# Activations and attention transposed in 32x32 blocks on VectorE and placed by DMA, in place of transposes on TensorE

## The chip, the core and the metric

The kernel runs on one core of one Trainium2 chip. The metric is device time in microseconds (us), median of several executions. Every execution told of here is marked fast in the record, and the results were correct. In both kernels TensorE (PE) multiplies into PSUM; VectorE (DVE) and ScalarE (ACT) evict PSUM and do elementwise work; GpSimd (POOL) does elementwise work in SBUF; all DMAs are issued, in order, from the queue of SyncE (SPq). Issue is the time that a DMA holds that queue; it has landed when its data may be read. A run of bytes is a contiguous piece that a DMA moves.

## The reference, cut to what matters

```python
h = relu(layernorm(x))                       # x: 128 batches x 64 tokens x 768, f32
for l in range(2):
    m_left, m_right = h @ W_left[l].T, h @ W_right[l].T
    u = (upper triangle of h @ m_left.T, lower triangle of h @ m_right.T) / sqrt(768)
    e = exp(u) * adj
    attention = e / (e.sum(2) + 1e-10)       # 64 x 64 per batch
    ctx = attention @ (h @ W_lin[l].T + b_lin[l])
    h = relu(layernorm_std(ctx) * ln_a[l] + ln_b[l])
return x + h
```

## The kernel before

Sixteen blocks of 512 tokens (8 batches) go through two passes per layer. Pass one needs `h` transposed (hidden index on partitions): it projects left and right in groups of seven products (Strassen-like sums of tokens and weights, PSUM banks X, Y, Z, V), and forms the scores and the attention. Pass two does the linear layer, the context and the layer norm.

The order of emission matters, since each engine runs its instructions in order (in block 0 VectorE stood 3.72 us for x, and TensorE 1.82 us for an eviction behind that). Side work is put in a queue of small closures, one of which is emitted after every product (`pump(1)`; an empty closure in the queue, an empty turn, a spacer, only delays what follows it):

```python
def project(u, k, g, between=None):
    for i, (at, a, t) in enumerate(ORDER):    # X Y Z V X Z V
        ...                                   # 3 matmuls into bank `at`
        if i == 0:   nc.scalar.copy(s1, p)
        elif i == 1: nc.vector.tensor_add(u2, p, s1)
        elif i == 2: nc.vector.tensor_add(u4, p, u2)      # bank Z is read here ...
        elif i == 4: nc.scalar.copy(to, pb)
        else:        nc.vector.tensor_add(to, pb, ...)    # ... and i == 5 adds into bank Z
        if i == 1 and between: between()      # scores(u - 1), queues its chain
        pump(1)

# per block, in pass one:
for g in range(CH):
    project(u, 0, g, (lambda: scores(u - 1)) if u and g == 0 else None)
    if g == 0:
        load(u + 1)                           # x (layer 0) or h (layer 1), adjacency
        prepare(u + 1)                        # queues the work on the next block
for g in range(CH): project(u, 1, g)

# prepare, layer 0: statistics and normalization on VectorE, then
for c in range(2):
    for q in range(Q):
        nc.tensor.transpose(p[:, c, q*P:(q+1)*P], xr[q][:, (c0+c)*P:(c0+c+1)*P], ident)
nc.scalar.activation(ht[:, c0:c0+2, :], p, AF.Relu)

# last links of the score chain (seven links): normalize, four transposes, one store
nc.tensor.transpose(pt[:, q, :], bd[:, q, :], ident)
nc.scalar.copy(at, pt)
nc.sync.dma_start(ATT[l][u], at)
```

In pass two of layer 0 each half block is transposed on TensorE, scaled and shifted by ScalarE on its way out of PSUM, and stored; pass one of layer 1 loads it as it needs it.

## Time and profile before

| | before |
|---|---|
| median time | 3039.55 us (3038.8 to 3040.02, 3 runs; 3039.78 with a fourth, run beside the changed kernel) |
| TensorE busy | 3001.1 us, 99% of the span |
| VectorE, ScalarE, GpSimd busy | 35%, 18%, 25% |
| mean granted TensorE clock | 0.998 |
| DMA packets | 77,994, 244.66 MB |

In a timeline line the first two numbers are start and duration in us; then engine, source line, operation, output and inputs, the number of instructions merged, and in brackets how long the engine had stood idle and what ended it.

### The profile page before, as it was taken

What the parts mean: (1) busy time and instruction counts of PE and PEld (TensorE: products, weight loads), DVE (VectorE), ACT (ScalarE), POOL (GpSimd) and SP (SyncE); (2) the same over time, 40 slices, a digit from 0 to 9 for tenths busy, and PEclk for the clock granted to TensorE, in tenths of its full rate; (3) what the DMA queues carried; (4) which work ended last, traced back from release to release, by engine and by line L of the source; (5) the groups of instructions that cost most, each with busy time, mean ns of one, the idle gap of its engine ahead of it and who ended that gap; (6) DMA issues with size and microseconds to landing.
All of it is one profiled execution on the core that took longest, in us unless ns stands there. A gap on an engine that the chain in (4) does not pass through costs nothing.

```text
span 3039.2 us, 37771 instructions
## 1 busy us (share of the span) xinstructions
PE 3001.1 (99%) x15744; PEld 2328.2 (77%) x15744; DVE 1061.3 (35%) x2231; ACT 551.6 (18%) x1124; POOL 765.5 (25%) x486
## 2 busy tenths in 40 slices
PE   7999999999999999999999999999999999999998
PEld 6888888888888755555568888888888886555554
DVE  4333333433333222222223222222222224555555
ACT  1112111121111144343431000000000001111111
POOL 3311211111112152322323111111111112555554
PEclk9999999999999999999999999999999999999999
DMA  4211211112111132222221010001000102444444
GB/s 173 80 56 49 90 49 49 56 49 91 49 49 61 53 152 111 98 107 111 90 90 60 29 56 28 28 29 56 28 28 29 56 28 100 152 177 153 177 152 139
DMA packets 77994, 244.66 MB, mean 81 GB/s; under 512 B 8448, under 2 KB 34560, under 8 KB 67584
## 3 DMA queue, kind: packets, MB, share of 16 engines
q1 hardware_dynamic: 77824, 242.25, 21.9%
q8 instruction: 124, 2.03, 0.3%
q14 instruction: 46, 0.38, 0.0%
HBM read 158.34 MB, written 83.89 MB: 80 GB/s over the span
## 4 chain that ended last, share of the span: by engine, by line
PE 97%; DVE 1%; DMA 1%; ACT 0%; issue 0%; POOL 0%; DVEq 0%; POOLq 0%; ACTq 0%; SPq 0%
PE Z L259 16%; PE V L259 16%; PE X L259 16%; PE Y L259 8%; PE Z L497 8%; PE V L497 8%; PE X L497 8%; PE aux L293 6%; PE Y L497 4%; PE aux L417 3%; PE aux L470 1%; PE aux L226 1%; PE aux L323 0%; DMA x<-in_x_dram 0%; DVE bd L317 0%
## 5 line engine op out<-in xcount | busy, mean ns | idle before, releaser
L135 POOL TENSOR_TENSOR ts<-ht 128x768 f32<-128x768 f32 x126 | 238.7, 1894 | 1541.3 <-ACT ht L228 742.7
L259 PE MATMUL X<-ht,w_l_A 128*128 128x256 f32 x1152 | 281.3, 380 | 0.0
L259 PE MATMUL V<-ts,w_l_A 128*128 128x256 f32 x1152 | 280.2, 379 | 0.5 <-DVE n L280 0.5
L259 PE MATMUL X<-ht,w_r_A 128*128 128x256 f32 x1152 | 280.0, 379 | 0.0
L259 PE MATMUL V<-ts,w_r_A 128*128 128x256 f32 x1152 | 280.0, 379 | 0.0
L497 PE MATMUL X<-w_n_A,ht 128*128 128x384 f32 x768 | 269.0, 486 | 0.3 <-DVE s L502 0.3
L497 PE MATMUL V<-w_n_A,ts 128*128 128x384 f32 x768 | 268.7, 486 | 0.0
L280 DVE TENSOR_TENSOR n<-V,u 128x256 f32<-128x256 f32 x384 | 162.3, 423 | 278.2 <-PE V L259 277.0
L259 PEld LDWEIGHTS X<-ht,w_r_A 128*128 128x128 f32 x1152 | 218.9, 190 | 29.8
L259 PEld LDWEIGHTS V<-ts,w_r_A 128*128 128x128 f32 x1152 | 218.9, 190 | 29.8
L135 POOL TENSOR_TENSOR ts<-ht,ts 128x768 f32<-128x768 f32 x126 | 239.3, 1899 | 7.7 <-ACT ht L228 6.4
L259 PEld LDWEIGHTS X<-ht,w_l_A 128*128 128x128 f32 x1152 | 218.4, 191 | 29.1
L259 PEld LDWEIGHTS V<-ts,w_l_A 128*128 128x128 f32 x1152 | 217.5, 190 | 30.0 <-DVE n L280 1.2
L273 DVE TENSOR_TENSOR u<-Y,s 128x256 f32<-128x256 f32 x192 | 81.5, 425 | 408.4 <-PE Y L259 408.4
L497 PEld LDWEIGHTS X<-w_n_A,ht 128*128 128x128 f32 x768 | 143.3, 190 | 94.0 <-DVE s L502 0.9
L497 PEld LDWEIGHTS V<-w_n_A,ts 128*128 128x128 f32 x768 | 143.5, 190 | 93.5
L280 DVE TENSOR_TENSOR n<-Z,u 128x256 f32<-128x256 f32 x192 | 80.8, 421 | 381.7 <-PE Z L259 381.7
L278 ACT COPY n<-X 128x256 f32<-128x256 f32 x192 | 71.5, 373 | 745.3 <-PE X L259 745.3
L435 ACT ACTIVATE z<-aux 128x768 f32<-128x768 f32 x128 | 102.6, 807 | 566.5 <-PE aux L417 566.5
L507 POOL TENSOR_TENSOR u2b<-u,b 128x384 f32<-128x384 f32 x64 | 63.8, 998 | 551.0 <-DVE u L505 551.0
L270 ACT COPY s<-X 128x256 f32<-128x256 f32 x192 | 71.5, 373 | 619.9 <-PE X L259 619.9
L293 PEld LDWEIGHTS aux<-n,ht 128*64 128x64 f32 x3072 | 167.0, 137 | 10.6 <-issue 10.6
(104 smaller groups left out, 4003.4 us busy)
## 6 DMA issues: line engine op xcount, KB each, us to landing
ht<-h SPq DMA_DIRECT2D x48, 1536.0 KB, 6.7
x<-in_x_dram SPq DMA_DIRECT2D x64, 384.0 KB, 7.2
h<-ht SPq DMA_DIRECT2D x16, 1536.0 KB, 6.1
h<-n SPq DMA_DIRECT2D x16, 1536.0 KB, 5.0
xr<-in_x_dram SPq DMA_DIRECT2D x64, 384.0 KB, 4.2
out_dram<-xr SPq DMA_DIRECT2D x64, 384.0 KB, 2.3
att<-at SPq DMA_DIRECT2D x32, 256.0 KB, 2.0
at<-att SPq DMA_DIRECT2D x32, 256.0 KB, 7.0
```

Source lines behind the costliest of these rows:

```text
L135: queue.append(lambda o=o, m=m, n=n: eng.tensor_sub(b[o], b[m], b[n]))
L226: nc.tensor.transpose(p[:, c, q * P:(q + 1) * P], xr[q][:, (c0 + c) * P:(c0 + c + 1) * P], ident)
L259: nc.tensor.matmul(p, w[a][:, c, g * P:(g + 1) * P], b[t][:, c, :], start=(new and c == 0), stop=(c == CH - 1), skip_group_check=True)
L270: nc.scalar.copy(s1, p)
L273: nc.vector.tensor_add(u2, p, s1)
L278: nc.scalar.copy(to, pb)
L280: nc.vector.tensor_add(to, pb, (u4 if i == 3 else u2).rearrange("p (b s) -> p b s", s=S))
L293: nc.tensor.matmul(p[h * S:(h + 1) * S, q, :], ht[:, c, b * S:(b + 1) * S], m[c // CH][:, c % CH, b].rearrange("p k j -> p (k j)"), start= ...
L417: nc.tensor.matmul(cx[k][i, m, :HH], at[j, q, j], hl[j, q, m * HH:(m + 1) * HH], start=True, stop=True)
L435: nc.scalar.activation(zs[k].rearrange(two, n=2), cx[k], AF.Square, accum_out=ss[:, k:k + 1])
L497: nc.tensor.matmul(p, b[t][:, c, r * P:(r + 1) * P], w[a][:, c, :], start=(new and c == 0), stop=(c == CH - 1), skip_group_check=True)
L507: nc.gpsimd.tensor_add(u2b, u2, rows["b2"])
```

## The change

The intent: TensorE is the bound, so take its 872 transposes off it. VectorE transposes 32x32 blocks, and DMAs to DRAM and back put the blocks in place. Only the first block of layer 0 keeps its TensorE transposes. The batches in a block are laid out anew so that the blocks fit.

```diff
+    def transpose_rows(l, u, pool):                  # layer 0 after statistics and relu
+        for q in range(Q):
+            queue.append(lambda q=q: nc.vector.transpose(
+                xb[:, :, q, :], xr[q].rearrange("p (b j) -> p b j", j=32)))
+        queue.append(store)                          # four DMAs, 512 byte runs
+        queue.append(lambda: load_h(1, l, u))        # one DMA back
+        queue.extend([lambda: None] * 4)             # four empty turns
+        affine(1, l, u)                              # layer 1: six ScalarE activations
...
-                    pt = ps_aux.tile(...)            # attention, last links
-                    for q in range(Q):
-                        nc.tensor.transpose(pt[:, q, :], bd[:, q, :], ident)
-                    nc.scalar.copy(at, pt)
-                    nc.sync.dma_start(ATT[l][u], at)
+                    nc.vector.transpose(at..., v...)
+                    for a in range(4):
+                        for g in range(2):
+                            nc.sync.dma_start(to[a // 2, a % 2, g], at[a * 32:(a + 1) * 32, g])
                 it = chain()
-                for _ in range(7):
+                for _ in range(6):
...
-                    nc.sync.dma_start(t, x_t[u][q])  # x: four DMAs of 128 partitions
+                    for a in range(4):               # eight DMAs of 32 partitions
+                        nc.sync.dma_start(t[a * 32:(a + 1) * 32], src.rearrange("(k j) h -> j k h", k=2))
...                                                  # pass two, layer 0
-                queue.append(lambda c0=c0: turn(c0)) # TensorE transposes, relu, store
+                nc.sync.dma_start(ROWS[u][batch(r, k, h)], zs[k][h * S:(h + 1) * S])
```

To make room, the difference buffers go from eight to six and some scratch from two to one; the normalization of layer 0 moves from VectorE to ScalarE.

More of the change, by code (lines that the diff above doesn't have):

```diff
@@ L63 @@
     ctx.enter_context(tc.manual_schedule())
-    x_t = x.rearrange("b s h -> (b s) h").rearrange("(n q p) h -> n q p h", q=Q, p=P)
-    out_t = out.rearrange("b s h -> (b s) h").rearrange("(n q p) h -> n q p h", q=Q, p=P)
-    adj_t = adj2.rearrange("b j k i -> (b j) (k i)").rearrange("(n q p) m -> n p q m", q=Q, p=P)
+    NBB = T // S
+    adj_t = adj2.rearrange("(n h s) j k i -> n h j s (k i)", h=PAIR, s=Q)
     queue = deque()
@@ L123, in tokens_of, with sub @@
     def tokens_of(key):
-        ht, ts = HT[key], TS[key]
+        ht = HT[key]
         r = {f"B{i + 1}{t + 1}": ht[:, i * CH:(i + 1) * CH, t * TH:(t + 1) * TH]
              for i in range(2) for t in range(2)}
-        r.update({f"T{i + 1}": ts[:, i] for i in range(4)})
+        r.update(TS.get(key, {}))
         return r
     def sums_t(key, eng=nc.gpsimd):
-        ts = big.tile([P, 4, CH, TH], F32, name="ts")
-        TS[key] = ts
-        b = tokens_of(key)
+        ts = TS[key] = {}
+        def sub(o, m, n):
+            ts[o] = big.tile([P, CH, TH], F32, name="ts", bufs=6)
+            b = tokens_of(key)
+            eng.tensor_sub(b[o], b[m], b[n])
         for o, m, n in (("T1", "B12", "B11"), ("T2", "B22", "T1"), ("T3", "B22", "B12"), ("T4", "B21", "T2")):
-            queue.append(lambda o=o, m=m, n=n: eng.tensor_sub(b[o], b[m], b[n]))
+            queue.append(lambda o=o, m=m, n=n: sub(o, m, n))
     def column(name, src):
@@ L140, in column @@
         return t
-    H0 = [dram.tile([P, C, T], F32, name=f"h0_{u}") for u in range(NB)]
-    H1 = [dram.tile([P, C, T], F32, name=f"h1_{u}") for u in range(NB)]
-    ATT = [[dram.tile([P, Q, P], F32, name=f"att{l}_{u}") for u in range(NB)] for l in range(L)]
+    KEPT = [[dram.tile([P, C, T], F32, name=f"h{l}_{u}") for u in range(NB)] for l in range(L)]
+    ROWS = [dram.tile([NBB, S, H], F32, name=f"z_{u}") for u in range(NB)]
+    ATT = [[dram.tile([P, Q, S], F32, name=f"att{l}_{u}") for u in range(NB)] for l in range(L)]
     ident = const.tile([P, P], F32, name="ident")
@@ L160 @@
     nc.vector.tensor_scalar(tri[:, 1, :], diff, 0.0, None, op0=ALU.is_gt)
-    BD = []
-    for i in range(2):
-        t = const.tile([P, Q, P], F32, name=f"bd{i}")
-        nc.gpsimd.memset(t, 0.0)
-        BD.append(t)
+    a_col, b_col = column("a_col", ln_a[0]), column("b_col", ln_b[0])
     def mean_var(mv, halves):
@@ L171, in mean_var, with load_rows, load_h @@
         nc.vector.bn_aggr(mv, st)
+    XR = {}
+    def load_rows(l, u, pool):
+        XR[l, u] = []
+        for g in range(2):
+            t = pool.tile([P, 2, H], F32, name="x", bufs=2)
+            for a in range(4):
+                i = 4 * g + a
+                src = x[u * NBB + i] if l == 0 else ROWS[u][i]
+                nc.sync.dma_start(t[a * 32:(a + 1) * 32], src.rearrange("(k j) h -> j k h", k=2))
+            XR[l, u].extend([t[:, 0, :], t[:, 1, :]])
+    def load_h(which, l, u):
+        ht = HT[which, l, u] = big.tile([P, C, T], F32, name="ht")
+        nc.sync.dma_start(ht, KEPT[l][u])
@@ new lines, in affine, with scale, norm, turn @@
+    def affine(which, l, u):
+        for c in range(C if l else 0):
+            queue.append(lambda c=c: nc.scalar.activation(
+                HT[which, l, u][:, c, :], HT[which, l, u][:, c, :], AF.Relu,
+                bias=b_col[:, c:c + 1], scale=a_col[:, c:c + 1]))
+    def transpose_rows(l, u, pool):
+        key, xr = (1, l, u), XR[l, u]
+        if l == 0:
+            mv = stat.tile([P, Q, 2], F32, name="mv0", bufs=2)
+            sd = stat.tile([P, Q], F32, name="sd0", bufs=2)
+            rs = stat.tile([P, Q], F32, name="rs0", bufs=2)
+            nb = stat.tile([P, Q], F32, name="nb0", bufs=2)
+            def scale(q0, q1):
+                nc.scalar.activation(sd[:, q0:q1], mv[:, q0:q1, 1], AF.Sqrt, bias=eps_in)
+                nc.vector.reciprocal(rs[:, q0:q1], sd[:, q0:q1])
+                nc.vector.scalar_tensor_tensor(nb[:, q0:q1], mv[:, q0:q1, 0], -1.0, rs[:, q0:q1],
+                                               op0=ALU.mult, op1=ALU.mult)
+            def norm(q):
+                nc.scalar.activation(xr[q], xr[q], AF.Relu, bias=nb[:, q:q + 1], scale=rs[:, q:q + 1])
+            for q in range(Q):
+                queue.append(lambda q=q: mean_var(mv[:, q, :], [xr[q][:, :HH], xr[q][:, HH:]]))
+                if u == 0:
+                    queue.append(lambda q=q: scale(q, q + 1))
+                    queue.append(lambda q=q: norm(q))
+            if u:
+                queue.append(lambda: scale(0, Q))
+                for q in range(Q):
+                    queue.append(lambda q=q: norm(q))
+        if (l, u) == (0, 0):
+            ht = HT[key] = big.tile([P, C, T], F32, name="ht")
+            def turn(c0):
+                p = ps_aux.tile([P, 2, T], F32, name="aux")
+                for c in range(2):
+                    for q in range(Q):
+                        nc.tensor.transpose(p[:, c, q * P:(q + 1) * P],
+                                            xr[q][:, (c0 + c) * P:(c0 + c + 1) * P], ident)
+                for c in range(2):
+                    nc.scalar.copy(ht[:, c0 + c, :].rearrange("p (a q j) -> p q a j", a=4, q=Q),
+                                   p[:, c].rearrange("p (q a j) -> p q a j", a=4, q=Q))
+            for c in range(0, C, 2):
+                queue.append(lambda c=c: turn(c))
+            queue.append(lambda: nc.sync.dma_start(KEPT[l][u], ht))
+            return
+        xb = pool.tile([P, H // 32, Q, 32], F32, name="n" if pool is big else "xb", bufs=2 if pool is big else 1)
+        def store():
+            to = KEPT[l][u].rearrange("(b i) c t -> i c b t", b=4)
+            for a in range(4):
+                nc.sync.dma_start(to[:, :, :, a * P:(a + 1) * P],
+                                  xb[a * 32:(a + 1) * 32].rearrange("i (c b) q j -> i c b (q j)", b=4))
+        for q in range(Q):
+            queue.append(lambda q=q: nc.vector.transpose(
[4 more added lines that the diff above has]
+        affine(1, l, u)
@@ L174, in pass_one @@
     def pass_one(l, aside):
         with tc.tile_pool(name=f"one{l}", bufs=2, reuse_waits="tile") as sp:
-            ADJ, WM, XR = {}, {}, {}
+            ADJ, WM = {}, {}
             def load(u):
-                if l == 0:
-                    XR[u] = []
-                    for q in range(Q):
-                        t = sp.tile([P, H], F32, name="x", bufs=4)
-                        nc.sync.dma_start(t, x_t[u][q])
-                        XR[u].append(t)
-                elif (1, l, u) not in HT:
-                    load_h(1, l, u)
-                ADJ[u] = sp.tile([P, Q, 2, S], F32, name="adj")
-                adj = ADJ[u].rearrange("p q k i -> p q (k i)")
-                if l == 0:
-                    nc.sync.dma_start(adj, adj_t[u])
-                else:
-                    nc.sync.dma_start(adj[:, :2], adj_t[u][:, :2])
-                    nc.sync.dma_start(adj[:S, 2:], adj_t[u][S:, 2:])
-                    nc.sync.dma_start(adj[S:, 2:], adj_t[u][:S, 2:])
+                if (l, u) not in XR:
+                    load_rows(l, u, sp)
+                ADJ[u] = sp.tile([P, Q, 2, S], F32, name="adj")
+                for h in range(PAIR):
+                    nc.sync.dma_start(ADJ[u][h * S:(h + 1) * S].rearrange("p s k i -> p s (k i)"), adj_t[u, h])
@@ L204, in prepare @@
             def prepare(u, eng=nc.gpsimd):
-                key = (1, l, u)
-                if l == 0:
-                    ht = big.tile([P, C, T], F32, name="ht")
-                    HT[key] = ht
-                    xr = XR[u]
-                    mv = stat.tile([P, Q, 2], F32, name="mv0", bufs=2)
-                    sd = stat.tile([P, Q], F32, name="sd0", bufs=2)
-                    rs = stat.tile([P, Q], F32, name="rs0", bufs=2)
-                    def scale(q0, q1):
-                        nc.scalar.activation(sd[:, q0:q1], mv[:, q0:q1, 1], AF.Sqrt, bias=eps_in)
-                        nc.vector.reciprocal(rs[:, q0:q1], sd[:, q0:q1])
-                    def norm(q):
-                        nc.vector.tensor_scalar(xr[q], xr[q], mv[:, q, 0:1], rs[:, q:q + 1],
-                                                op0=ALU.subtract, op1=ALU.mult)
-                    def turn(c0):
-                        p = ps_aux.tile([P, 2, T], F32, name="aux")
-                        for c in range(2):
-                            for q in range(Q):
-                                nc.tensor.transpose(p[:, c, q * P:(q + 1) * P],
-                                                    xr[q][:, (c0 + c) * P:(c0 + c + 1) * P], ident)
-                        nc.scalar.activation(ht[:, c0:c0 + 2, :], p, AF.Relu)
-                    for q in range(Q):
-                        queue.append(lambda q=q: mean_var(
-                            mv[:, q, :], [xr[q][:, :HH], xr[q][:, HH:]]))
-                        if u == 0:
-                            queue.append(lambda q=q: scale(q, q + 1))
-                            queue.append(lambda q=q: norm(q))
-                    if u:
-                        queue.append(lambda: scale(0, Q))
-                        for q in range(Q):
-                            queue.append(lambda q=q: norm(q))
-                    for c in range(0, C, 2):
-                        queue.append(lambda c=c: turn(c))
-                    queue.append(lambda: nc.sync.dma_start(H0[u], ht))
-                if key not in TS:
-                    sums_t(key, eng)
+                if (1, l, u) not in TS:
+                    transpose_rows(l, u, sp)
+                    sums_t((1, l, u), eng)
                 queue.append(lambda: masks(u))
@@ L268, in project @@
                     if i == 0:
-                        s1 = sp.tile([P, TH], F32, name="s1")
+                        s1 = sp.tile([P, TH], F32, name="s1", bufs=1)
                         nc.scalar.copy(s1, p)
                     elif i == 1:
-                        u2 = sp.tile([P, TH], F32, name="u2")
+                        u2 = sp.tile([P, TH], F32, name="u2", bufs=1)
                         nc.vector.tensor_add(u2, p, s1)
                     elif i == 2:
-                        u4 = sp.tile([P, TH], F32, name="u4")
+                        u4 = sp.tile([P, TH], F32, name="u4", bufs=1)
                         nc.vector.tensor_add(u4, p, u2)
@@ L313, in chain @@
                     nc.vector.reciprocal(s, s)
-                    bd = BD[u % 2]
-                    for h in range(PAIR):
-                        r = slice(h * S, (h + 1) * S)
-                        nc.vector.tensor_tensor(bd[r, :, r], v[r], s[r].unsqueeze(2).to_broadcast([S, Q, S]),
-                                                op=ALU.mult)
-                    yield
-                    yield
-                    pt = ps_aux.tile([P, 2, T], F32, name="aux")[:, 0].rearrange("p (q m) -> p q m", q=Q)
-                    for q in range(Q):
-                        nc.tensor.transpose(pt[:, q, :], bd[:, q, :], ident)
-                    at = stat.tile([P, Q, P], F32, name="at", bufs=1)
-                    nc.scalar.copy(at, pt)
-                    nc.sync.dma_start(ATT[l][u], at)
+                    nc.vector.tensor_tensor(v, v, s.unsqueeze(2).to_broadcast([P, Q, S]), op=ALU.mult)
+                    yield
+                    at = sp.tile([P, 2, Q, 32], F32, name="at", bufs=1)
+                    nc.vector.transpose(at.rearrange("p g q i -> p q g i"),
+                                        v.rearrange("p q (g j) -> p q g j", g=2))
+                    to = ATT[l][u].rearrange("(b g j) q (h i) -> b h g j q i", b=2, g=2, h=2)
+                    for a in range(4):
+                        for g in range(2):
+                            nc.sync.dma_start(to[a // 2, a % 2, g], at[a * 32:(a + 1) * 32, g])
                 it = chain()
-                for _ in range(7):
+                for _ in range(6):
                     queue.append(lambda: next(it, None))
@@ L358, in pass_one @@
                             load_h(2, l, 0)
+                            queue.extend([lambda: None] * 4)
+                            affine(2, l, 0)
                             sums_t((2, l, 0))
@@ L365, in pass_one @@
             scores(NB - 1)
-            flush(keep=1)
-    def load_h(which, l, u):
-        ht = big.tile([P, C, T], F32, name="ht")
-        nc.sync.dma_start(ht, (H0 if l == 0 else H1)[u])
-        HT[which, l, u] = ht
+            flush()
     def pass_two(l, aside):
@@ L395, in pass_two @@
                 row("b", ln_b[l])
-            else:
-                a_col = column("a_col", ln_a[l])
-                b_col = column("b_col", ln_b[l])
-            AT, XR, HL, OUT, Z = {}, {}, {}, {}, {}
+            AT, HL = {}, {}
             def load(u):
@@ L403, in load @@
                     load_h(2, l, u)
-                AT[u] = sp.tile([P, Q, P], F32, name="at", bufs=3)
+                AT[u] = sp.tile([P, Q, S], F32, name="at", bufs=3)
                 nc.sync.dma_start(AT[u], ATT[l][u])
@@ L416, in context, with batch @@
                         m = n if j == lo else 1 - n
-                        nc.tensor.matmul(cx[k][i, m, :HH], at[j, q, j], hl[j, q, m * HH:(m + 1) * HH],
+                        nc.tensor.matmul(cx[k][i, m, :HH], at[j, q, :], hl[j, q, m * HH:(m + 1) * HH],
                                          start=True, stop=True)
                 return [c[:, :, :HH] for c in cx]
+            def batch(r, k, h):
+                return 4 * (h if k == 0 else 1 - h) + r + 2 * k
             def finish(u, r):
                 cx = context(u, r)
-                zs = [sp.tile([P, H], F32, name="z", bufs=2) for _ in range(2)]
+                zs = [sp.tile([P, H], F32, name="z", bufs=2 if last else 4) for _ in range(2)]
                 xs = []
@@ L427, in finish @@
                         xr = sp.tile([P, H], F32, name="xr", bufs=2)
-                        nc.sync.dma_start(xr, x_t[u][r + 2 * k])
+                        for h in range(PAIR):
+                            nc.sync.dma_start(xr[h * S:(h + 1) * S], x[u * NBB + batch(r, k, h)])
                         xs.append(xr)
@@ L448, in done @@
                         nc.vector.scalar_tensor_tensor(xs[k], zs[k], 0.0, xs[k], op0=ALU.max, op1=ALU.add)
-                        nc.sync.dma_start(out_t[u][r + 2 * k], xs[k])
+                        for h in range(PAIR):
+                            nc.sync.dma_start(out[u * NBB + batch(r, k, h)], xs[k][h * S:(h + 1) * S])
                     queue.append(lambda: scaled(0))
@@ L456, in finish, with scaled @@
                     return
-                if r == 0:
-                    OUT[u] = big.tile([P, C, T], F32, name="n")
-                ho = OUT[u].rearrange("p c (t r i) -> p c t r i", t=2, r=2)
-                def scaled():
-                    for k in range(2):
-                        nc.scalar.activation(zs[k].rearrange(two, n=2), cx[k], AF.Copy, scale=rs[:, k:k + 1])
-                def turn(c0):
-                    p = ps_aux.tile([P, 2, T], F32, name="aux")
-                    for c in range(2):
-                        for t in range(2):
-                            nc.tensor.transpose(p[:, c, t * P:(t + 1) * P],
-                                                zs[t][:, (c0 + c) * P:(c0 + c + 1) * P], ident)
-                    for c in range(2):
-                        nc.scalar.activation(ho[:, c0 + c, :, r, :],
-                                             p[:, c, :2 * P].rearrange("p (t i) -> p t i", t=2), AF.Relu,
-                                             bias=b_col[:, c0 + c:c0 + c + 1],
-                                             scale=a_col[:, c0 + c:c0 + c + 1])
-                queue.append(scaled)
-                queue.append(lambda: None)
-                for c0 in range(0, C, 2):
-                    queue.append(lambda c0=c0: turn(c0))
-                if r == 1:
-                    queue.append(lambda: nc.sync.dma_start(H1[u], OUT[u]))
+                def scaled(k):
+                    nc.scalar.activation(zs[k].rearrange(two, n=2), cx[k], AF.Copy, scale=rs[:, k:k + 1])
+                    for h in range(PAIR):
+                        nc.sync.dma_start(ROWS[u][batch(r, k, h)], zs[k][h * S:(h + 1) * S])
+                queue.append(lambda: scaled(0))
+                queue.append(lambda: scaled(1))
             def linear(u, r, before, aside):
@@ L531, in pass_two @@
                         before = lambda: finish(*((u, 0) if r else (u - 1, 1)))
+                    kept = list(queue)
+                    queue.clear()
                     beside = deque()
+                    nxt = (2, l, u + 1) if u + 1 < NB else None if last else (1, 1, 0)
                     if r == 0:
@@ L535, in pass_two @@
                             load(u + 1)
-                        elif not last:
-                            load_h(1, 1, 0)
+                            affine(*nxt)
+                        elif nxt:
+                            load_rows(1, 0, sp)
+                            transpose_rows(1, 0, big)
+                        if u + 1 < NB:
+                            queue.extendleft([lambda: None] * (7 - len(queue)))
                         if u in aside:
@@ L540, in pass_two @@
                     else:
-                        kept = list(queue)
-                        queue.clear()
-                        if u + 1 < NB:
-                            sums_t((2, l, u + 1))
-                        elif not last:
-                            sums_t((1, 1, 0))
+                        if nxt:
+                            sums_t(nxt)
                         if u in aside:
                             loaded()
-                        beside.extend(queue)
-                        queue.clear()
-                        queue.extend(kept)
+                    beside.extend(queue)
+                    queue.clear()
+                    queue.extend(kept)
                     linear(u, r, before, beside)
```

## The prediction

> **What bounds the kernel now.** I read the page first (busy time, chain), then the chain in order of time, then the timeline of one block of 512 tokens. Busy shares and the chain of work that ended last:
>
> ```profile
> PE 3001.1 (99%) x15744; PEld 2328.2 (77%) x15744; DVE 1061.3 (35%) x2231; ACT 551.6 (18%) x1124; POOL 765.5 (25%) x486
> ...
> PE 97%; DVE 1%; DMA 1%; ACT 0%; issue 0%; POOL 0%; DVEq 0%; POOLq 0%; ACTq 0%; SPq 0%
> PE Z L259 16%; PE V L259 16%; PE X L259 16%; PE Y L259 8%; PE Z L497 8%; PE V L497 8%; PE X L497 8%; PE aux L293 6%; PE Y L497 4%; PE aux L417 3%; PE aux L470 1%; PE aux L226 1%; PE aux L323 0%; DMA x<-in_x_dram 0%; DVE bd L317 0%
> ```
>
> TensorE is the bound: no other engine holds a per cent. L226, L470 and L323 are its transposes. What one costs on the path is read where only transposes differ: two-product stretches of the second pass, layer 0 against layer 1, in the chain in order of time:
>
> ```profile
> 1046.65 2.13 PE Y L497 x6
> 1063.16 2.13 PE Y L497 x6
> 1079.67 2.13 PE Y L497 x6
> ...
> 2648.31 2.13 PE Y L497 x6
> 2678.70 2.13 PE Y L497 x6
> ```
>
> A block (two such lines) takes 33.02 us in layer 0 and 30.39 us in layer 1. The 2.63 us between them are 24 transposes, so 0.110 us each (their own 277 ns overlap).
>
> Whether VectorE has slack is a question of its order, not of its 35%. In the timeline of block 0 of layer 0, the one block whose x was not loaded far ahead:
>
> ```profile
> 24.77 2.54 SPq L183 DMA_DIRECT2D x<-in_x_dram  x4
> ...
> 33.76 1.02 DVE L170 BATCH_NORM_STATS2 st<-x 128x6 f32<-128x384 f32 x2 [3.72 <-DMA x<-in_x_dram]
> ...
> 37.45 0.37 DVE L276 TENSOR_TENSOR u<-Z,u 128x256 f32<-128x256 f32 x1
> ...
> 37.87 1.56 PE L259 MATMUL Z<-ht,w_l_S 128*128 128x256 f32 x6 [1.82 <-DVE u L276]
> ```
>
> VectorE stood 3.72 us for x, the PSUM evictions behind it came late, and TensorE stood 1.82 us for one (the next product, too, started late). So a VectorE instruction that waits for a DMA does stop TensorE. In every later block x is loaded half a block ahead, and VectorE does not wait:
>
> ```profile
> 97.91 1.01 DVE L170 BATCH_NORM_STATS2 st<-x 128x6 f32<-128x384 f32 x2
> ...
> 115.86 3.58 SPq L183 DMA_DIRECT2D x<-in_x_dram  x4
> ```
>
> [...] No transposition of VectorE is in this trace. [...] the DVE's queue is one in-order queue; the 3.72 us above agree. [...] a DMA behind a waiting one waits too; the waits of the DMA queue (491 us of it for an eviction of the mask product) agree. [...] the attention's new stores have 128 B runs, the activations' 512 B. The trace has no 128 B store to compare.
>
> **The change part by part.**
>
> *Removed.* Transposes: 360 of 384 of x, all 384 of the hidden rows, all 128 of attention: 872 x 0.110 = **96 us**, all on the path. Without new waits: 3039.5 - 96 = 2943.5 us. The evictions of the transposes leave ScalarE, which is no bound (18%).
>
> *Added on VectorE.* 128 transpositions of 128x768 and 32 of 128x256. I take [...] as VectorE's own 128x768 subtraction (954 ns) did: about 0.85 to 0.95 us, some 120 us in all, against 43 us of normalization that leave. 35% becomes about 38%: hidden, as a sum.
>
> *The moved wait on x (first stall).* From the order of instructions: before, the attention store stood behind the x load on the DMA queue; now eight attention stores stand ahead of the eight x loads, and they wait for the attention's transposition, the last link of the score chain, popped with product 6 of the block's first group. VectorE's very next instruction reads x (statistics in layer 0, transposition in layer 1). I place this on the timeline of the block whose scores start at 82.30. Transposition of attention ends about 95.3 (the eviction of 94.80, earlier by the second normalization that goes, plus 0.42). Eight stores of 128 descriptors at about 0.42 us of issue (adjacency loads 0.38 to 0.61, attention 0.33): 98.7. Four x loads at 0.45 (1.81 us for four at the start): 100.5. Landing some 2 us after: 102.5. Then VectorE does statistics, eviction, statistics, eviction: 2 x (1.02 + 0.21) + 2 x 0.42 = 3.3: 105.8. The product into Z that waits for that second eviction would start at 100.74. **Stall 5.1 us** a block in layer 0, 14 blocks: 71 us. In layer 1 two transpositions stand for the statistics: 2.65 us, stall 4.4 us, 14 blocks: 62 us.
>
> *The round trip through DRAM (second stall, layer 1).* The transposed blocks are stored, read back and, in layer 1, scaled and shifted by six ScalarE activations, the first queued six products after the store, ahead of the eviction of the second X product (from the order on ScalarE). TensorE needs that eviction nine products after the stalled Z product: 9 x 1.295 = 11.65 us (products follow each other at 1.295 us). The last transposition ends about 2.2 us after the Z product's start; store S; load 6.9 (median now 6.7); one activation and the eviction 0.87. Stall = 2.2 + S + 6.9 + 0.87 - 11.65 = S - 1.7. Whole-block stores now take 5.0 to 6.1 us with 12 KB runs; with 512 B runs in four DMAs I choose S = 8. **Stall 6.3 us**, 14 blocks: 88 us; block 0 about 4. In layer 0 only GpSimd waits for the load: its differences are due some 10 us later, so no stall.
>
> *Once.* The start has more DMAs ahead of x and its chain goes over ScalarE (+3 us); between the layers the first block's round trip holds ScalarE's share of the last block (+5 us).
>
> *Sum.* 2943.5 + 71 + 62 + 88 + 4 + 8 = 3176.5; I say 3172, since each stall eases the next block's DMA a little.
>
> **The rivals.** (1) All hidden: 2944 us. For it: DMA engines at 22%, VectorE at 35%, spacers queued before the activations. Against it: the stall of block 0 above, which is this very pattern. The first stall cannot be under 3 us even with 0.33 us issues and 1 us landings. (2) The first stall only, the store as quick as now (S = 5 and less before it): 2944 + 133 + 28 to 46, some 3110 us. (3) VectorE's transposition at half my rate: two more of 0.9 us in each first stall of layer 1, and attention's 0.4 in both: +40 us; 3215. (4) Small runs choke the DMA (S = 12): +56 us. (5) GpSimd becomes late: six difference buffers in place of eight let the third and fourth difference start only when the block's last group has read the old ones; from there to the use some 9 us plus the scores, for 3.8 us of work (two at 1.9). Hidden.
>
> **Range and chances.** Rival 2, with stalls 1 us shorter, gives the low end, about 3085; rivals 3 and 4 in part the high end, 3245. Below 2979 nearly all stalls must be absent: 4%. Between 2979 and 3100: 12%. Above: 84%.
>
> **What would show it.** The chain of waits should have TensorE's Z product waiting for VectorE's eviction 4 to 5 us in 28 blocks, VectorE waiting for x about 7 us in the same blocks, and in layer 1 ScalarE waiting for ht, then X products for ScalarE, about 6 us. Transposes of TensorE: 24. The second pass of layer 0 should fall to 30.4 us a block: the part of the gain that is kept. Wrong: x landing before VectorE asks for it; a round trip under 11 us; a transposition far from 0.9 us; or stalls in the second passes.

## The result, and the profile after

The changed kernel takes **3446.56 us** (3445.75 to 3452.11, 4 runs) against 3039.78 us before: ratio 1.1343, 95% interval 1.1323 to 1.1362. A ratio is the mean time of one kernel's fast runs over that of the other's of the same rounds, so not quite the ratio of the medians. The direction was forecast, the size was not: +407 us against a forecast +132. All outputs are right.

The page of the changed kernel, busy time, granted clock over 40 slices of the span (in tenths), and the chain that ended last:

```profile
PE 3020.3 (88%) x14872; PEld 2310.3 (67%) x14872; DVE 1142.9 (33%) x2310; ACT 586.5 (17%) x1114; POOL 770.7 (22%) x484
...
PEclk9998999989999999999898999998898889999999
...
PE 16%; DMA 1%; SPq 1%; POOL 0%; DVE 0%; issue 0%; ACT 0%; DVEq 0%; POOLq 0%; ACTq 0%
```

TensorE fell from 99% to 88%. It issues 872 instructions fewer and is nevertheless busy 19 us longer, and the granted clock dips; its mean is 0.937. (The last chain is followed only as far back as it could be, 16% of the span, so the waits in total are the better view.)

```profile
PE Z L301 <- DVE u L318: 251.4, 30, 11.5
...
DVE st L174 <- DMA x<-in_x_dram: 181.6, 29, 12.2
...
DVE xb L257 <- DMA x<-z: 127.2, 24, 11.6
...
PE X L301 <- ACT n L320: 111.8, 15, 8.9
```

These are who waited for whom, us in total, times, longest. TensorE stood 251 us for VectorE's eviction of Z in 30 places and 112 us for ScalarE's eviction of X in 15: the two stalls of the prediction, both larger. The first of them in the timeline of a block of layer 0 (its score products start at 89.09):

```profile
101.60 0.43 DVE L360 STREAM_TRANSPOSE at<-v 128x256 f32<-128x256 f32 x1
102.06 5.06 SPq L365 DMA_DIRECT2D att<-at  x8
...
107.22 3.82 SPq L188 DMA_DIRECT2D x<-in_x_dram  x8
...
113.25 1.02 DVE L174 BATCH_NORM_STATS2 st<-x 128x6 f32<-128x384 f32 x2 [11.21 <-DMA x<-in_x_dram]
...
115.90 0.37 DVE L318 TENSOR_TENSOR u<-Z,u 128x256 f32<-128x256 f32 x1
116.32 2.93 PE L301 MATMUL Z<-ht,w_l_S 128*128 128x256 f32 x6 [8.62 <-DVE u L318]
...
119.04 2.60 PE L301 MATMUL V<-ts,w_l_A 128*128 128x256 f32 x6
...
121.48 1.46 PE L301 MATMUL X<-ht,w_l_A 128*128 128x256 f32 x6
```

Eight stores hold the DMA queue 5.06 us, x comes 6.0 us after its first load was issued, VectorE waits 11.21 us, TensorE 8.62 us. And then something that was not forecast: the product after the stall takes 2.93 us and the next 2.60, where 1.46 is usual (the third is again). The windows of this stretch (columns: length, busy time of TensorE, its weight loads, VectorE, ScalarE, GpSimd, then granted clock, DMA share, GB/s) show why:

```profile
108.00:116.00 8.00, 0.00 (x0) 0.00 (x0) 2.68 (x8) 1.39 (x2) 0.00 (x0) 0.69 0.97 209
116.00:120.00 4.00, 3.68 (x9) 2.96 (x10) 2.99 (x9) 0.30 (x1) 0.00 (x0) 0.50 1.09 331
120.00:124.00 4.00, 4.00 (x17) 3.42 (x16) 1.03 (x4) 2.62 (x4) 0.00 (x0) 0.83 0.81 301
124.00:140.00 16.00, 16.00 (x76) 14.09 (x75) 7.50 (x14) 2.66 (x5) 0.00 (x0) 1.00 0.39 92
```

The clock had fallen to 0.50 by the end of the idle time and stayed there for the first 4 us of work. In windows of 1 us it falls just after 111 us, some 3.4 us after the last product had ended (107.70), and reads 1.00 again from 122, some 5 us after work began. The prediction had not looked at the clock.

How slow it is varies. Products usually follow each other at 1.295 us. The first product after each of the 44 waits of 5.8 to 11.5 us in this kernel's first passes takes 2.93 us, the second between 1.53 and 2.77, the third at most 1.86. From start to start these make 103 us more than usual, beside 362 us of waiting. The clock reads 1.00 again 3.0 to 6.3 us after work began, in windows of 0.25 us.

The second stall, in a block of layer 1:

```profile
2012.66 5.22 SPq L253 DMA_DIRECT2D h<-xb  x4
...
2023.10 0.34 SPq L193 DMA_DIRECT2D ht<-h  x1
2029.93 0.81 ACT L198 ACTIVATE ht<-ht,b_col,a_col 128x512 f32<-128x512 f32 x1 [14.51 <-DMA ht<-h]
2030.65 0.35 ACT L320 COPY n<-X 128x256 f32<-128x256 f32 x1
...
2031.06 2.93 PE L301 MATMUL X<-ht,w_r_A 128*128 128x256 f32 x6 [8.27 <-ACT n L320]
2033.78 2.67 PE L301 MATMUL Y<-ts,w_r_S 128*128 128x256 f32 x6
```

Store 10.4 us, load 6.8, ScalarE 14.51 us idle with an eviction behind it, TensorE 8.27 us, and again two slow products.

The cleanest measure of a block is the time from its first score matmul to that of the next one, read from TensorE's timeline. Means of the 14 full blocks of each layer's first pass; "first" and "second" say which stall a kernel still has:

| kernel | median us | layer 0, us a block | layer 1, us a block |
|---|---|---|---|
| before | 3039.78 | 63.1 | 60.8 |
| after (first, second) | 3446.56 | 71.9 | 80.5 |
| x early (second) | 3157.46 | 60.1 | 71.5 |
| activations late (first) | 3306.57 | 71.9 | 71.4 |
| both | 2984.78 | 60.1 | 60.1 |
| both and the seams | 2956.75 | 60.1 | 60.1 |
| busy in first stall | 3450.30 | 71.3 | 80.9 |
| busy in second stall, x early | 3128.49 | 60.1 | 69.4 |
| stores doubled | 3600.95 | 76.6 | 85.6 |
| attention alone | 3180.50 | 71.6 | 60.8 |
| activations alone | 3114.16 | 60.8 | 67.9 |
| x in four DMAs | 3696.41 | 78.7 | 89.5 |
| attention in four DMAs | 3452.40 | 72.0 | 81.0 |

### The profile page after: what moved, and what is told of

The parts are those of the page before. It is cut to its first block, busy times and chain, and to the rows that moved or that the text cites. A ratio compares the mean times of both kernels' runs of the same rounds, so it can differ in the third digit from the quotient of the medians.

```text
span 3445.2 us, 37340 instructions
## 1 busy us (share of the span) xinstructions
PE 3020.3 (88%) x14872; PEld 2310.3 (67%) x14872; DVE 1142.9 (33%) x2310; ACT 586.5 (17%) x1114; POOL 770.7 (22%) x484
## 5 line engine op out<-in xcount | busy, mean ns | idle before, releaser
L301 PE MATMUL Z<-ht,w_l_S 128*128 128x256 f32 x576 | 182.6, 464 | 250.5 <-DVE u L318 250.5
L301 PE MATMUL X<-ht,w_r_A 128*128 128x256 f32 x1152 | 302.0, 401 | 111.8 <-ACT n L320 111.8
L301 PEld LDWEIGHTS X<-ht,w_r_A 128*128 128x128 f32 x1152 | 229.5, 201 | 150.6 <-ACT n L320 117.8
L301 PEld LDWEIGHTS Z<-ht,w_l_S 128*128 128x128 f32 x576 | 130.0, 232 | 283.0 <-DVE u L318 262.1
L301 PE MATMUL V<-ts,w_l_A 128*128 128x256 f32 x1152 | 306.0, 406 | 0.3 <-DVE n L322 0.3
L301 PEld LDWEIGHTS V<-ts,w_l_A 128*128 128x128 f32 x1152 | 239.7, 208 | 40.5 <-DVE n L322 1.7
L198 ACT ACTIVATE ht<-ht,b_col,a_col 128x512 f32<-128x512 f32 x192 | 142.2, 804 | 328.0 <-DMA ht<-h 328.0
L312 ACT COPY s<-X 128x256 f32<-128x256 f32 x192 | 71.4, 372 | 738.9 <-PE X L301 732.8
```

Source lines behind the costliest of these rows:

```text
L198: queue.append(lambda c=c: nc.scalar.activation(HT[which, l, u][:, c, :], HT[which, l, u][:, c, :], AF.Relu, bias=b_col[:, c:c + 1], scale ...
L301: nc.tensor.matmul(p, w[a][:, c, g * P:(g + 1) * P], b[t][:, c, :], start=(new and c == 0), stop=(c == CH - 1), skip_group_check=True)
```

## The experiments

The theory: the transposes' 96 us are gained, and lost to two waits that are a matter of order on in-order queues, each followed by a stretch at half clock. Rivals: DMAs choked by short runs; VectorE's transpositions themselves; for the slow products, memory traffic in place of the clock. Before ran beside every group of runs (the groups ran on different chips), with medians between 3039.2 and 3044.1 us.

**x early.** The rows of the next block are loaded at the start of a block, ahead of the attention stores:

```diff
+                if u and u + 1 < NB:
+                    load_rows(l, u + 1, sp)
                 for g in range(CH):
                     project(u, 0, g, ...)
```

> The changed kernel with the eight x loads of the next block moved on the DMA queue from behind the eight attention stores to the start of the block. Theory (the order on the DMA queue makes VectorE wait for x): VectorE's wait for x (309 us in the changed kernel) falls under 20 us, TensorE's wait for VectorE's eviction (251 us) under 20 us, and the slow products after it (about 68 us) go too; with 1 to 2 us less of the second stall in layer 1, about 3105 us. Rival (the DMA engines are choked by small runs, so x comes late wherever it is issued): x still lands after VectorE asks, over 3300 us.

Measured: 3157.46 us, ratio 1.0388 (1.0373 to 1.0404). The first stall is gone, in its waits and in the blocks of layer 0 (60.1 us). In the timeline of the same block as above, the statistics now run beside the stores:

```profile
102.42 0.98 DVE L174 BATCH_NORM_STATS2 st<-x 128x6 f32<-128x384 f32 x2
102.52 5.07 SPq L365 DMA_DIRECT2D att<-at  x8
```

The theory holds; the short runs are still there and hurt nothing in layer 0. It was 52 us slower than expected, since the second stall did not shrink: 71.5 us a block where the expectation amounts to some 68, and its wait rose from 111.8 to 133.3 us. The transpositions end earlier, but the store is issued about 1 us after the last of them, when the queue is done with the attention stores and the adjacency, and the load back takes 8.0 us for 6.8, with the next block's x issued right behind it.

**Activations late.** In layer 1 twelve empty turns in place of four between load and activations:

```diff
-        queue.extend([lambda: None] * 4)
+        queue.extend([lambda: None] * (12 if l else 4))
```

> The changed kernel with twelve spacers in place of four between the load of the transposed block and ScalarE's six activations in layer 1. Theory (ScalarE waits for the round trip and holds the eviction of X): TensorE's wait for ScalarE (112 us) goes and the slow products after it (about 36 us): about 3298 us, the first stall unchanged at 251 us. Rival (GpSimd's differences then come too late): a new wait of TensorE for GpSimd at the start of each block of layer 1, and no gain.

Measured: 3306.57 us, ratio 1.0874 (1.0858 to 1.0891), as the theory had it. The second stall was the place of the activations in ScalarE's order. GpSimd was not late: no wait of TensorE for it is in the profile.

**Both.**

> Both edits together. Theory (two stalls and the slow clock after each are the whole loss): 2944 us plus some 30 us at the start and between the passes, about 2975 us, granted clock 0.99 or more. Rival (VectorE's transpositions or the extra DMA cost of themselves): over 3040 us.

Measured: 2984.78 us, ratio 0.9818 (0.9804 to 0.9833), clock 0.992. All transpositions, stores and loads of the change are in this kernel, and it is 1.8% faster than before (the interval is clear of 1): they cost little of themselves, and the block is 60.1 us in both layers. So the first stall costs 3306.57 - 2984.78 = 322 us alone (11.5 us in each of 28 blocks), the second 3157.46 - 2984.78 = 173 us alone, and together 462 us: 33 us less than their sum. Part of that is to be expected, since each slow product after the first stall gives the second's DMAs time; it was not measured by itself.

**Busy in the first stall.** Seventeen matmuls that nobody reads are put before the product that stalls:

```diff
+                    if i == 5 and k == 0 and g == 1 and 0 < u < NB - 1:
+                        idle = ps_aux.tile([P, 2, T], F32, name="aux")
+                        for _ in range(17):
+                            nc.tensor.matmul(idle[:, 0, :TH], w["A11"][:, 0, :P], b["B11"][:, 0, :], start=True, stop=True)
```

> The changed kernel with 17 matmuls whose result nobody reads (7.3 us of TensorE work) put in front of the product that stalls 8 to 11 us in each block. Theory (an idle TensorE is granted half the clock [...]): the stall is filled, the products after it run at 1.3 us in place of 2.3 to 2.9, and the kernel with more work is about 68 us faster, 3378 us. Rival (the products after the stall are slow because DMA and VectorE crowd the memory at that moment): they stay slow, 3446 us or more.

Measured: 3450.30 us, ratio 1.1358 (1.1339 to 1.1377): no gain, so the forecast of time failed, though the clock rose from 0.937 to 0.969. The same block in its timeline:

```profile
108.56 7.50 PE L303 MATMUL aux<-ht,w_l_A 128*128 128x256 f32 x34
...
118.00 1.56 PE L306 MATMUL Z<-ht,w_l_S 128*128 128x256 f32 x6 [1.94 <-DVE u L323]
...
119.88 1.56 PE L306 MATMUL V<-ts,w_l_A 128*128 128x256 f32 x6 [0.31 <-DVE n L327]
```

In this block the products do run at full speed (1.56 us in place of 2.93), with the same DMAs and the same VectorE work beside them, so here the rival on memory traffic falls. But the filler did this in 7 of the 14 blocks of layer 0 only. In the others 2.1 to 5.3 us of waiting were left behind it, and one of the two products or both stayed slow, as here:

```profile
192.75 2.93 PE L306 MATMUL Z<-ht,w_l_S 128*128 128x256 f32 x6 [5.30 <-DVE u L323]
195.47 2.72 PE L306 MATMUL V<-ts,w_l_A 128*128 128x256 f32 x6
```

Where did the rest of the gain go? Three things are in the traces. First, x came later: VectorE first read it 12.3 us after the attention's transposition began, on average over 28 blocks, for 11.8 (in the block at 118.00 it was 0.66 us later, with its loads' issue lasting 4.87 us for 3.82). Second, V then waits for VectorE, which has more statistics ahead of V's eviction: even in the seven good blocks X starts 3.2 to 4.0 us after Z, where 2.59 is usual and 5.16 was measured in the changed kernel's block above. So part of what the slow clock takes here would be lost to VectorE at full clock too. Third, in layer 1 the second stall takes what is left (80.9 us a block against 80.5). Why x comes later is open.

**Busy in the second stall.** The same filler in the run with x early, before the X product of the second projection's first group in layer 1.

> The run with x early and 17 unread matmuls (7.3 us) in front of the X product that waits about 9 us for ScalarE in each block of layer 1. This stall's end is set by a DMA and ScalarE alone, and nothing but TensorE gates the two products after it. Theory (they run at half clock because TensorE was idle): blocks of layer 1 shrink from 71.5 to about 69.2 us, 3123 us in all. Rival (they are slow for another reason, or the filled stall grows as the first one did): blocks stay at 71.5 us, 3157 us.

Measured: 3128.49 us, ratio 1.0285 (1.0268 to 1.0303), 29 us less than without the filler (two groups of runs, with before at 3044 and 3041 us), and 69.4 us a block for 71.5, as expected. Here the products after the filler are at full speed in all blocks but two.

```profile
1748.50 7.50 PE L303 MATMUL aux<-ht,w_r_A 128*128 128x256 f32 x34
...
1757.49 1.56 PE L306 MATMUL X<-ht,w_r_A 128*128 128x256 f32 x6 [1.48 <-ACT n L325]
```

More work, less time: an idle TensorE costs more than the idle time. How long a wait is too long? In these first passes, waits up to 2.0 us left the products at full speed (1.56 us), unless a slow product came just before (with x in four DMAs, below, V took up to 2.93 us after waits of 1.0 to 1.6 us behind a slow Z); after every wait of 4.0 us or more (the run with the activations alone has 14 of 4.0 to 4.9 us) the first product took 2.9 us. Between these both occur: here 3.5 us left the products alone in one block and 2.2 us did not in another.

**Stores doubled.** Every attention store is issued twice.

> The changed kernel with every attention store issued twice, so the stores occupy the DMA queue some 10 us in place of 5.06 before the x loads. Theory (the first stall is additive in the time of that issue): 28 blocks longer by about 5 us each, 3586 us. Rival (x lands late for another reason, the issue being hidden): under 3490 us.

Measured: 3600.95 us, ratio 1.1831 (1.1813 to 1.1849); blocks 4.7 and 5.1 us longer.

```profile
101.99 10.20 SPq L366 DMA_DIRECT2D att<-at  x16
...
112.29 3.82 SPq L188 DMA_DIRECT2D x<-in_x_dram  x8
...
118.02 1.02 DVE L174 BATCH_NORM_STATS2 st<-x 128x6 f32<-128x384 f32 x2 [16.06 <-DMA x<-in_x_dram]
```

The issue ahead of x grew by 5.1 us and so, nearly, did the block: what is issued ahead of x is stall. x comes 5.7 us after its first load is issued, much as without the doubling (6.0), so the extra short runs do not slow x itself.

**Attention alone.** The kernel before, with only the attention's part of the change.

> The kernel before with the attention part of the change alone: VectorE transposes, eight stores, which stand ahead of the next block's x on the DMA queue. Theory (the loss of layer 0 is the place of these stores on the queue, whoever transposes the activations): blocks of layer 0 lengthen from 63.1 to about 72 us, with VectorE waiting for x in 14 blocks; blocks of layer 1, where no VectorE instruction reads what is loaded behind the stores, stay at 60.4 to 61.3; about 3160 us. Rival (the first stall comes from the activations' transpositions): about 3025 us, faster by the 128 transposes alone.

Measured: 3180.50 us, ratio 1.0463 (1.0447 to 1.0478). Layer 0 has the first stall without any transposition of activations (71.6 us a block); layer 1 has none (60.0 us in all blocks but one of 71.5 us, in which VectorE waits 7.9 us for weights of the linear layer that are loaded behind the stores: the same pattern). The theory holds. Here x is still loaded by four DMAs of 128 partitions and VectorE's first statistics need only the first of them, 384 KB: it read 3.4 us after that was issued (172.60 to 176.03 in the timeline). In the changed kernel its first read needs four DMAs of 32 partitions, 768 KB, and came after 6.0 us. So the new layout of x would account for 2.6 us of the stall (an estimate, 6.0 - 3.4); this compares two kernels, and the run made to test it (x in four DMAs, below) could not show it.

**Activations alone.** The changed kernel with the attention's part undone.

> The changed kernel with attention transposed on TensorE again and stored by one DMA (and a single zeroed buffer for it, which is all that fits), so x is loaded ahead of that store. Theory: no first stall, the second stall as in the run with x early: blocks of layer 0 about 60.6 us, of layer 1 about 72 us, 3171 us. Rival (the DMA round trip and the transpositions delay x by themselves): blocks of layer 0 stay over 65 us.

Measured: 3114.16 us, ratio 1.0242 (1.0224 to 1.0259). No first stall, as the theory has it (60.8 us in layer 0). Layer 1 is better than expected, 67.9 us for 72. The attention's chain has seven links again, so the activations come one product later and fall behind the eviction of X; the next eviction that they hold, s for the following group, is needed four products later. TensorE waits 66 us for that one in place of 133.

**x in four DMAs** of 128 partitions, each taking 32 tokens of four batches.

> The changed kernel with x loaded by four DMAs of 128 partitions in place of eight of 32. Theory (the first stall is as long as the issue of the stores, the issue of the x loads and their landing): about 1 us less of issue and 1 us less of landing for the first pair, so 2 us less in each of 28 blocks: about 3390 us. Rival (only the eight stores ahead set it): 3446 us.

Measured: 3696.41 us, ratio 1.2164 (1.2145 to 1.2182): a miss, the wrong way. The windows after the issue of the x loads, of this run and of the changed kernel (the adjacency's loads begin within the last 1 to 2 us of each):

```profile
122.00:126.00 4.00, 0.47 (x3) 0.07 (x1) 0.00 (x0) 1.66 (x2) 0.00 (x0) 1.00 0.21 47
```

```profile
107.50:113.00 5.50, 0.20 (x1) 0.00 (x0) 0.00 (x0) 1.66 (x2) 0.00 (x0) 0.83 0.85 194
```

DMA share 0.21 against 0.85, and 47 GB/s against 194. Why these loads move at about a quarter of the rate was not shown: no run shows the single engines. The experiment changed the rate of the transfer with the count of DMAs, and says nothing on the count.

**Attention in four DMAs** of 64 partitions.

> The changed kernel with the attention stored by four DMAs of 64 partitions in place of eight of 32, the same bytes in the same 128 byte runs. If the 5.06 us that the stores occupy the DMA queue go by the number of DMAs: 2.5 us less in each of 28 blocks, about 3376 us. If they go by the number of runs: no change, 3446 us.

Measured: 3452.40 us, ratio 1.1364 (1.1347 to 1.1381). The four stores hold the queue 4.20 us where eight held it 5.06, and the x loads behind them take 4.69 us to issue for 3.82: 0.86 us less and 0.87 us more. Inconclusive: why the loads take longer to issue was not shown.

**Both and the seams.** The run with both edits, and waits of the same kind taken out of the start and the places where passes meet: bias rows loaded one block ahead of their use, the scale and shift columns loaded after the weights, layer 1's first block transposed and stored a block earlier, eight empty turns before the activations at the end of a first pass.

> The run with both edits, and the same done at the seams: the linear bias rows loaded in the last block of each first pass, the two columns for scale and shift loaded after the weights, the first block of layer 1 transposed and stored one block earlier, four spacers more before the activations at the end of the first pass. Theory (what is left over 2944 us are waits of the same kind at the start and the seams, 41 us): about 28 us less than the run with both edits, 2957 us. Rival (the rest is spread cost of the extra DMA traffic): 2975 us or more.

Measured: **2956.75 us** (2955.61 to 2960.97), ratio 0.9717 (0.9703 to 0.9732), clock 0.996. This beats both kernels, and is 13 us over the 2943.5 us of the prediction's sum without waits.

```profile
PE 2908.2 (98%) x14872; PEld 2242.8 (76%) x14872; DVE 1144.6 (39%) x2310; ACT 585.5 (20%) x1114; POOL 770.8 (26%) x484
```

## Why the prediction was right or wrong

- **TensorE as the bound and 96 us of transposes: right.** A block fell to 60.1 us in layer 0 in the run with both edits, and the last run comes within 13 us of the floor. The second pass of layer 0 fell to 30.39 us a block in the changed kernel, as forecast.
- **VectorE's transpositions hidden as a sum: right.** They took 964 ns against an estimated 850 to 950, and VectorE is 39% busy in the last run against a forecast 38%. (The estimate rested on the 954 ns of one subtraction of 128x768; with the 416 ns of an addition of 128x256 the trace before shows 1.05 ns an element between them. And 124 blocks of 128x768 were transposed so, not 128, since the first block kept TensorE.)
- **What failed, in the sum: the lengths of the two stalls, and the time after them.** The sum has 225 us of stalls (71 + 62 + 88 + 4); the changed kernel waits 362 us in these places, and runs slow products for 103 us more, for which the sum has no term.
- **First stall, the mechanism: right; the size: wrong.** Forecast 5.1 and 4.4 us a block; the waits are 9.1 and 8.4 us on average, and 11.5 us of time were lost. The terms, from the block of layer 0 above: "about 0.42 us of issue" a store measured 0.63, which makes 5.06 us for 3.4. Four x loads and "some 2 us" to landing, 3.8 us in the forecast, measured 6.0 (the 2 us were the author's estimate; median times from issue to landing in the trace before are 2.0 us for the attention's stores and 7.2 us for x). VectorE's part was 3.0 for 3.3. That makes 8.6 us of waiting. The remaining 2.6 us or so in this block is Z and V run slowly.
- **No term for the clock.** The sum took TensorE to run at full rate as soon as it may run. At least the first product after each stall ran at half rate (2.93 us for 1.46, at a granted clock of 0.50); Z and V above take 5.16 us from start to start where 2.59 is usual. The run with the second stall filled shows that it is the idle time that makes them slow: the filler adds work to TensorE and to no other engine, and the products behind it run at full speed. How much the clock costs after the first stall was not isolated, since VectorE holds V there.
- **Second stall, the mechanism: right; the size: wrong.** "I choose S = 8": the store took 10.4 us, 5.22 of it issue of four DMAs of 768 runs. From the first activation to the product it was 1.13 us for 0.87. The last transposition ended 3.2 us after the Z product's start for 2.2, and the nine products took 13.3 us for 11.65, since the slow Z is among them. 3.2 + 10.4 + 6.8 + 1.1 - 13.3 = 8.2, against a wait of 8.27 in this block. Alone (x early) the wait was 8.9 us on average and with the slow products 11.4 us a block, for 6.3.
- **Rivals.** (1), all hidden, (2), a second stall of 2 to 3.3 us, (3), slow transpositions, and (5), GpSimd late, did not occur. (4), DMAs choked by short runs, has something in it: the store's 10.4 us lie between the 8 chosen and its 12. But in the run with both edits, with the same short runs, it costs nothing in the block. No rival had a clock in it, yet that alone did not put the result over the high end of 3245: the run with both edits plus the waits that it does not have would be some 3340 us (2985 + 356, an estimate).
- **Seams: right in kind.** 8 us were forecast, and 4 in block 0; the run with both edits stands 41 us over the floor, and mending the seams takes 28 us of it away.
- **A reading.** The 491 us that the queue waits "for an eviction of the mask product" are waits for VectorE's product with the adjacency (line 308). That a waiting DMA holds those behind it stands all the same: in the trace before the adjacency's load waited 36.2 us and was issued at 91.40, and the loads of the linear weights behind it, into buffers not used before, at 91.83.

Open: why x came later while TensorE was kept busy in the first stall, how much of the slow products after the first stall would remain with VectorE's wait, why the x loads by four DMAs moved at a quarter of the rate, and whether fewer, larger attention stores would shorten the stall if the x loads behind them were issued as fast as before.

## What to carry to other kernels

When work moves off the bound engine onto in-order engines and DMAs, go through each queue in order and ask, for each instruction that will wait for a DMA, what stands behind it that the bound engine needs; here the shares of busy time (VectorE 33%) told nothing, and moving one load and adding eight empty turns turned 13% slower into 1.8% faster. Price a stall of the bound engine by more than its length: after waits of 4 us and more TensorE ran at half clock as well, 103 us on top of 362 us here. And measure a merge of DMAs before counting on it: x in four DMAs in place of eight moved at 47 GB/s for 194, and the kernel was 250 us slower.

## Times of issue, landing and transposition measured here

- The time of issue on the queue, by shape: 0.63 us for a store of 128 runs of 128 B from 32 partitions, 0.48 us for a load of 64 runs of 3 KB, 1.3 us for a store of 768 runs of 512 B, 0.34 to 0.45 us for whole-tile DMAs of 128 runs (in the trace before, 0.34 of att at 96.81 and 0.45 of x at 0.74). Nor does shape alone fix it: eight loads of 64 runs took 3.82 us in the changed kernel and 7.82 with x early, behind a load of 1.5 MB.
- Landing, in two kernels: the first 768 KB by four DMAs of 32 partitions were there after 6.0 us, the first 384 KB by one DMA of 128 partitions after 3.4 us, with three more behind it.
- VectorE's transpositions of f32: 24 x 4 blocks (128x768) took 964 ns, 128x256 took 0.43 us.
